# Graph attention layer with residual and layer norm, fp32: products of W and `a` spread over 14 steps, and blocks of rows that lie 32 apart

## The chip, the cores and the metric

One Trainium2 chip, one core. The time is the device time of one execution in microseconds (us), and each kernel has a median over three runs. The profile is of one further execution, with an own time and an own span (first to last instruction).

## What is computed

x is 4096 x 512, adj 4096 x 4096, W 512 x 2048 (four heads of 512), all fp32. Cut to what matters:

```python
ht = (h @ W).reshape(N, N_HEADS, N_HIDDEN).transpose(1, 0, 2)
src = jnp.einsum('hnd,hd->hn', ht, a_src)
dst = jnp.einsum('hnd,hd->hn', ht, a_dst)
e = jax.nn.leaky_relu(src[:, :, None] + dst[:, None, :], SLOPE) + adj_mat[None]
att = jax.nn.softmax(e, axis=-1)
h_prime = jnp.einsum('hij,hjd->hid', att, ht)
x = _layernorm(x + h_prime.mean(axis=0), axis=-1)
```

The entries of adj that are not zero are uniform up to 1e9, so in almost every row one entry leads the others by far more than the scores can differ. The softmax of such a row is 1 at that column, and its result is the layer norm of `x[i] + x[col(i)] @ mean over heads of W`.

## The kernel before, in words

`leading_rows` computes this short form for all rows, and a bound that proves it valid (or not) for each row. `general`, the full attention, is behind a branch on that bound; no instruction of it stands in the profiled execution.

The rows are worked on in 32 blocks of 128, one row in each of the 128 partitions; block `ib` holds rows 128*ib to 128*ib+127 (`adj_rows`, `x_rows` and `out_rows`, lines 87 to 90). A tile of adj, `adj_t`, is 128 rows of 4096 (2 MB); six buffers exist and loads run five blocks ahead (`AHEAD`). x lies in `hold`, and the result is written over it; its upper half (blocks 16 to 31) first holds W, so x groups 4 to 7 (four blocks each) can only be loaded when W has been used. A load of x takes 2 KB from each of four blocks per partition.

The loop over `t` (line 321) has one step per block. In one step:

- SP issues the load of adj for block t+5, at the steps in `x_at` a group of x before it. All loads of adj, W and x and nearly all stores stand in SP's one queue; the stores of finished groups come after the last load.
- VectorE (DVE) reduces the adj tile to 64 segment maxima in two halves (`segment_maxima`, L151). Between the halves stands `find_column` of block t-2 (it reads the gathered `lead`, and POOL then gathers the rows `y` of x), and at even t from 6 on the reciprocal of `rstd` (L213 on ScalarE, L214 and L215 on DVE) for blocks t-6 and t-5. After the second half `find_segment` finds the leading segment, and POOL gathers it (`lead`, 256 bytes a row).
- TensorE (PE) and ScalarE (ACT): `head_vector` (`vectors_at`: four at t=1 and at t=2, one at each of t=3 to 10) turns a 128 x 512 piece of W (four transposes L255), ACT copies it (`wt`, L257), and four thin products give `pv` (L259). `project` of block t-3 puts x into the accumulator `o` (L191), transposes y (L194), ACT copies (`yt`, L196), and four products with `w_sum`, the mean of the heads, add to `o` (L198). Then ACT does `finish` of two blocks (even t), `stats` of block t-4 (L208, L210) and `row_norm` (L203).

The order on every engine is the order in which the code is written (`tc.manual_schedule()`); each engine works strictly through its own list. A `rstd` on DVE at step t waits for `stats` of block t-5, which ACT did in step t-1, behind the `yt` copy of block t-4.

At t=0 PE forms `w_sum` from W (L238). After the loop stand the last columns, `test` (L296) with one product on PE, the projects of blocks 29 to 31, and the last stores.

Of the kernel before, what the change touches and what calls it, by code (L numbers as in the profile page):

```python
# [9 lines left out]
F32 = mybir.dt.float32  # L10
# [9 lines left out]
P = 128  # L20
C = 512
# [44 lines left out]
def leading_rows(ctx, tc, x, adj, W, a, out, ident, v, n_bad, any_bad):  # L66
# [3 lines left out]

    nc = tc.nc
    N, D = x.shape
    H = a.shape[0]
    KB, NB, S = D // P, N // P, N // E
    AHEAD = 5
    Q = 4
# [5 lines left out]
    rows = ctx.enter_context(tc.tile_pool(name="rows", bufs=2))  # L84
    psum = ctx.enter_context(tc.tile_pool(name="psum", bufs=4, space=bass.MemoryType.PSUM))

    adj_rows = adj.rearrange("(nb p) m -> nb p m", p=P)
    adj_segs = adj.rearrange("n (s e) -> (n s) e", e=E)
    x_rows = x.rearrange("(nb p) d -> p nb d", p=P)
    out_rows = out.rearrange("(nb p) d -> p nb d", p=P)  # L90
    w_blocks = W.rearrange("(kb p) (h d) -> p kb h d", p=P, h=H)

    hold = once.tile([P, NB, D], F32, name="hold")
# [31 lines left out]

    make_identity(nc, ident)
    first_i = once.tile([P, NB], I32, name="first_i")
    nc.gpsimd.iota(first_i, pattern=[[P * S, NB]], base=0, channel_multiplier=S)
    first = once.tile([P, NB], F32, name="first")
    nc.gpsimd.tensor_copy(first, first_i)  # L130
    ones = once.tile([P, P], F32, name="ones")
# [26 lines left out]
    def find_segment(ib):  # L158
        seg = seg_of.pop(ib)
        nc.vector.max(out=top[:, ib, :], in_=seg)  # L160
        at = small.tile([P, 8], U32, name="at")
        nc.vector.max_index(at, top[:, ib, :], seg)
        row = small.tile([P, 1], U32, name="row")
        nc.vector.tensor_tensor(row, at[:, 0:1], first[:, ib : ib + 1], op=OP.add)  # L164
        lead = small.tile([P, E], F32, name="lead")
        nc.gpsimd.indirect_dma_start(  # L166
            out=lead, out_offset=None, in_=adj_segs,
            in_offset=bass.IndirectOffsetOnAxis(ap=row[:, :1], axis=0),
        )
        at_of[ib], lead_of[ib] = at, lead  # L170
# [14 lines left out]
        )  # L185
        y_t[ib] = y

    def project(ib):
        y = y_t.pop(ib)
        o = psum.tile([P, D], F32, name="o")  # L190
        nc.tensor.matmul(o, ident, hold[:, ib, :], start=True, stop=False)  # L191
        tp = psum.tile([P, KB, P], F32, name="tp", bufs=2)
        for kb in range(KB):
            nc.tensor.transpose(tp[:, kb, :], y[:, ts(kb, P)], ident)  # L194
        yt = rows.tile([P, KB, P], F32, name="yt")
        nc.scalar.copy(yt, tp)  # L196
        for kb in range(KB):
            nc.tensor.matmul(o, yt[:, kb, :], w_sum[:, kb, :], start=False, stop=(kb == KB - 1))  # L198
        o_ps[ib] = o

    def row_norm(ib):
        sq = rows.tile([P, D], F32, name="sq")
# [9 lines left out]
    def rstd(i):  # L212
        nc.scalar.activation(sd[:, i], sd[:, i], AF.Sqrt, bias=eps, scale=1.0 / D)  # L213
        nc.vector.reciprocal(sd[:, i], sd[:, i])  # L214
        nc.vector.tensor_mul(nm[:, i], nm[:, i], sd[:, i])  # L215
# [32 lines left out]
            nc.tensor.transpose(tp[:, k, : 2 * H], a_rows[:, ts(k, P)], ident[: 2 * H, : 2 * H])  # L248
        nc.scalar.copy(at_d, tp[:, :, : 2 * H])

    def head_vector(kb, h):

        tp = psum.tile([P, KB, P], F32, name="tp", bufs=2)
        for k in range(KB):
            nc.tensor.transpose(tp[:, k, :], hold[:, w_at + kb * H + h, ts(k, P)], ident)  # L255
        wt = rows.tile([P, KB, P], F32, name="wt")
        nc.scalar.copy(wt, tp)  # L257
        for k in range(KB):
            nc.tensor.matmul(  # L259
                pv[:, kb, h : 2 * H : H], wt[:, k, :], at_d[:, k, h : 2 * H : H],  # L260
                start=(k == 0), stop=(k == KB - 1),
            )
# [47 lines left out]
        nc.vector.tensor_reduce(total, pg, axis=AX.X, op=OP.add)  # L310
        nc.vector.tensor_scalar(any_bad, total, -1.0, float(N), op0=OP.mult, op1=OP.add)

    x_at = {1: 1, 3: 2, 6: 3, 12: 4, 14: 5, 17: 6, 20: 7}
    norms_at = {t: [t - 2] for t in range(2, 18)}
    for k in range(8):
        norms_at[18 + k] = [16 + 2 * k, 17 + 2 * k]
    vectors = [(kb, h) for kb in range(KB) for h in range(H)]
    vectors_at = {1: 4, 2: 4, **{t: 1 for t in range(3, 11)}}
    COLUMN, PROJECT, STATS, FINISH = 2, 3, 4, 6

    for t in range(NB):
        if t in x_at:
            load_x(x_at[t])
        load_adj(t + AHEAD)
        segment_maxima(t, 0)
        if t >= COLUMN:
            find_column(t - COLUMN)
        if t >= FINISH and t % 2 == 0:
            rstd(slice(t - FINISH, t - FINISH + 2))
        segment_maxima(t, 1)  # L330
        find_segment(t)
        if t == 0:
            for kb in range(KB):
                mean_of_heads(kb)
            turn_a()
        for _ in range(vectors_at.get(t, 0)):
            head_vector(*vectors.pop(0))
        if t == 11:
            head_norms()
        if t >= PROJECT:  # L340
            project(t - PROJECT)
        if t >= FINISH and t % 2 == 0:
            finish(t - FINISH)
            finish(t - FINISH + 1)
        if t >= STATS:
            stats(t - STATS)
        for ib in norms_at.get(t, ()):
            row_norm(ib)
        if 27 <= t <= 29:
            bound(t - 27)  # L350

    find_column(NB - 2)
    find_column(NB - 1)
# [4 lines left out]
        store(nc.sync, g * Q, Q)  # L358
    test()
    for ib in range(NB - PROJECT, NB):  # L360
        project(ib)
        stats(ib - 1)
        rstd(slice(ib - 1, ib))
        finish(ib - 1)
        if ib == NB - 2:
            store(nc.sync, NB - Q, 2)
# [6 lines left out]
def general(ctx, tc, x, adj, W, out, ident, v, n_bad):  # L373
# [19 lines left out]
    w_blocks = W.rearrange("(kb p) m -> p kb m", p=P)  # L393

    with ExitStack() as pre:
        two = pre.enter_context(tc.tile_pool(name="two", bufs=2))
        pps = pre.enter_context(tc.tile_pool(name="pps", bufs=2, space=bass.MemoryType.PSUM))
        for g in range(NCH):
            nc.sync.dma_start(x_sb[:, ts(g, Q), :], x_blocks[:, ts(g, Q), :])
        for kb in range(KB):  # L400
            nc.sync.dma_start(w_sb[:, kb, :], w_blocks[:, kb, :])
        for g in range(NCH):
            xT = two.tile([P, KB, C], F32, name="xT")
            for q in range(Q):
                ps = pps.tile([P, KB, P], F32, name="ps_x")
                for kb in range(KB):
                    nc.tensor.transpose(ps[:, kb, :], x_sb[:, g * Q + q, ts(kb, P)], ident)
                nc.scalar.copy(xT[:, :, ts(q, P)], ps)
            ps = pps.tile([2 * H, C], F32, name="ps_sd")
            for kb in range(KB):  # L410
                nc.tensor.matmul(ps, v[:, kb, :], xT[:, kb, :], start=(kb == 0), stop=(kb == KB - 1))
            sd = two.tile([2 * H, C], F32, name="sd")
            nc.vector.tensor_copy(sd, ps)
            for h in range(H):
                pb = pps.tile([P, C], F32, name="ps_b")
                one_hot = ident[: 2 * H, H + h : H + h + 1].to_broadcast([2 * H, P])
                nc.tensor.matmul(pb, one_hot, sd, start=True, stop=True)
                nc.vector.tensor_copy(dst_b[:, h, ts(g, C)], pb)
            pt = pps.tile([P, Q, 2 * H], F32, name="ps_s")
            for q in range(Q):  # L420
                nc.tensor.transpose(pt[:, q, :], sd[:, ts(q, P)], ident[: 2 * H, : 2 * H])
            nc.vector.tensor_copy(src[:, ts(g, Q), :], pt[:, :, :H])

    adj_pool = ctx.enter_context(tc.tile_pool(name="adj_g", bufs=1))
# [7 lines left out]
    def block(ib):  # L432
        adj_t = []
        for k in range(NCH // AW):
            t = adj_pool.tile([P, AW * C], F32, name=f"adj{k}")
            nc.sync.dma_start(t, adj[ds(ib * P, P), ts(k, AW * C)])
            adj_t.append(t)
        src_i = stat.tile([P, H], F32, name="src_i", bufs=1)
        nc.vector.tensor_copy(src_i, src[:, ds(ib, 1), :].rearrange("p o h -> p (o h)"))
# [2 lines left out]
        class Unit:  # L442
# [65 lines left out]
            def project(self):  # L508
                h = self.h
                if h == 0:  # L510
                    held["o"] = psum.tile([P, D], F32, name="o_ps", bufs=1)
                for kb in range(KB):
                    nc.tensor.matmul(
                        held["o"], self.yt[:, kb, :], w_sb[:, kb, ts(h, D)],
                        start=(h == 0 and kb == 0), stop=(h == H - 1 and kb == KB - 1),
                    )

        def finish():
            r = y_pool.tile([P, D], F32, name="y_g")
            nc.vector.tensor_add(r, held["o"], x_sb[:, ds(ib, 1), :].rearrange("p o d -> p (o d)"))  # L520
            st = stat.tile([P, nc.vector.BN_STATS_DIM], F32, name="st_g")
            nc.vector.bn_stats(st, r)
            mv = stat.tile([P, nc.vector.BN_AGGR_DIM], F32, name="mv_g")
            nc.vector.bn_aggr(mv, st)
            sd = stat.tile([P, 1], F32, name="sd_g")
            nc.vector.tensor_scalar_add(sd, mv[:, 1:2], EPS)
            nc.scalar.activation(sd, sd, AF.Sqrt)
            nc.vector.reciprocal(sd, sd)
            nc.vector.tensor_scalar(r, r, mv[:, 0:1], sd, op0=OP.subtract, op1=OP.mult)
            nc.sync.dma_start(out[ds(ib * P, P), :], r)  # L530

        u = Unit(0)
        for c in range(NCH):
# [66 lines left out]
```

## Time and profile before

| | us |
|---|---|
| median of three runs (283.83, 280.98, 283.46) | 283.46 |
| the profiled execution | 282.4 |
| its span | 280.5 |
| PE busy | 220.3 |
| DVE busy | 192.1 |
| ACT busy | 120.7 |

The DMA engines moved 97.75 MB in the span, 348 GB/s on average. The mean granted clock of TensorE was 0.921 of 2.4 GHz.

How to read the rows further below: busy time alone says little, because stages have different limits. A row of the timeline gives start, duration, engine and operation, and in brackets how long the engine stood idle before it and what released it. The chain of waits follows the last instruction back to what released it, step by step; a row is start, duration and what ran. A group of instructions ends with the idle time before its members and the releaser.

### The profile page before, as it was taken

Reading aid. Unit: us, or ns where it says so; the run is one execution under the profiler, and the core shown is the slowest. Engines: PE = TensorE matmul, PEld = TensorE weight load, DVE = VectorE, ACT = ScalarE, POOL = GpSimd, SP = SyncE. Lnnn points to the kernel's source line nnn. Section 1 sums busy time; section 2 is a strip of 40 time slices with the busy share of each in tenths; the row PEclk is TensorE's granted clock in tenths of the full one; section 3 lists DMA queues with packets and bytes.
Section 4 is the critical chain, followed back from the end, with each engine's and each line's share of the span. In section 5 each row is a group of like instructions: output and inputs, shape, how many; then the busy total and the mean of one; then the engine's idle time right before and its main releaser. Section 6 shows DMA issues by size and latency. Waiting matters only on the chain.

```text
span 280.5 us, 2442 instructions
## 1 busy us (share of the span) xinstructions
PE 220.3 (79%) x683; PEld 112.6 (40%) x684; DVE 192.1 (68%) x381; ACT 120.7 (43%) x295; POOL 61.8 (22%) x75
## 2 busy tenths in 40 slices
PE   0389877778888888889987879887999789888980
PEld 0134666654444444434433333433444334343430
DVE  2524878840029695888999999599879999983011
ACT  1010211211465455365453735674566434465540
POOL 1101123310002222122332332232322322232000
PEclk9999755559999999999999997999899979999997
DMA  7999999999999979499999999999999999415121
GB/s 232 436 416 425 418 425 393 430 400 435 430 409 402 388 289 408 154 416 409 409 426 421 408 418 426 407 418 428 420 355 361 329 408 407 152 42 162 67 101 59
DMA packets 18147, 97.75 MB, mean 348 GB/s; under 512 B 1992, under 2 KB 1992, under 8 KB 13776
## 3 DMA queue, kind: packets, MB, share of 16 engines
q1 hardware_dynamic: 14384, 87.82, 77.9%
q0 software_dynamic: 3584, 9.44, 9.2%
q10 hardware_dynamic: 160, 0.28, 0.3%
q8 instruction: 7, 0.11, 0.2%
q14 instruction: 12, 0.10, 0.1%
HBM read 89.15 MB, written 8.39 MB: 348 GB/s over the span
## 4 chain that ended last, share of the span: by engine, by line
PE 43%; DMA 19%; DVE 18%; ACT 12%; issue 5%; ACTq 0%; POOLq 0%
PE o L198 19%; DVE seg L151 13%; DMA y<-in_x_dram,col 11%; PE pv L259 8%; DMA hold<-in_L_gnn_W_dram 6%; PE o L191 5%; ACT yt L196 4%; PE tp L255 4%; PE tp L194 3%; ACT wt L257 3%; PE o L238 3%; ACT sq L210 2%; DMA adj_t<-in_adj_dram 2%; ACT sq L203 2%; ACT sq L208 1%
## 5 line engine op out<-in xcount | busy, mean ns | idle before, releaser
L151 DVE TENSOR_REDUCE seg<-adj_t 128x32 f32<-128x2048 f32 (+1 forms) x68 | 146.2, 2153 | 22.9 <-DMA adj_t<-in_adj_dram 22.8
L198 PE MATMUL o<-w_sum,yt 128*128 128x512 f32 x256 | 123.4, 627 | 21.6 <-ACT yt L196 21.6
L198 PEld LDWEIGHTS o<-w_sum,yt 128*128 128x128 f32 x256 | 47.8, 197 | 78.5 <-issue 49.1
L196 ACT COPY yt<-tp 128x512 f32<-128x512 f32 x32 | 18.7, 585 | 86.0 <-PE tp L194 86.0
L166 POOL DMA_INDIRECT lead<-in_adj_dram,row x32 | 30.3, 948 | 107.8 <-DVE row L164 99.7
L182 POOL DMA_INDIRECT y<-in_x_dram,col x32 | 30.2, 944 | 85.7 <-issue 62.7
L214 DVE RECIPROCAL sd<-sd 128x2 f32<-128x2 f32 (+1 forms) x17 | 2.8, 163 | 48.7 <-ACT sd L213 48.6
L191 PE MATMUL o<-hold,ident 128*128 128x512 f32 x64 | 34.6, 623 | 0.0
L259 PE MATMUL pv<-at_d,wt 128*128 128x2 f32 x128 | 23.4, 304 | 11.3 <-ACT wt L257 11.3
L259 PEld LDWEIGHTS pv<-at_d,wt 128*128 128x128 f32 x128 | 22.0, 259 | 16.3 <-ACT wt L257 16.3
L238 PE MATMUL o<-hold,ident 128*128 128x512 f32 x32 | 15.6, 646 | 13.1 <-DMA hold<-in_L_gnn_W_dram 13.1
L194 PEld LDWEIGHTS tp<-ident,y 128*128 128x128 f32 x128 | 15.8, 143 | 25.2 <-issue 25.0
L194 PE MATMUL tp<-ident,y 128*128 128x128 f32 x128 | 19.9, 279 | 5.9 <-DMA y<-in_x_dram,col 5.9
L257 ACT COPY wt<-tp 128x512 f32<-128x512 f32 x16 | 9.4, 586 | 34.6 <-PE tp L255 34.6
L219 ACT ACTIVATE hold<-o,nm,sd 128x512 f32<-128x512 f32 x31 | 22.7, 780 | 3.0 <-DVE nm L215 3.0
L210 ACT ACTIVATE sq<-o,nm 128x512 f32<-128x512 f32 x31 | 21.3, 687 | 1.0
L203 ACT ACTIVATE sq<-hold 128x512 f32<-128x512 f32 x32 | 19.7, 619 | 0.0
L208 ACT ACTIVATE sq<-o 128x512 f32<-128x512 f32 x31 | 18.7, 603 | 0.0
L191 PEld LDWEIGHTS o<-hold,ident 128*128 128x128 f32 x64 | 11.5, 195 | 10.0 <-issue 9.9
L238 PEld LDWEIGHTS o<-hold,ident 128*128 128x128 f32 x32 | 6.5, 209 | 21.1 <-issue 18.9
L255 PE MATMUL tp<-ident,hold 128*128 128x128 f32 x64 | 13.3, 346 | 0.0
L239 ACT ACTIVATE w_sum<-o 128x512 f32<-128x512 f32 x4 | 2.4, 597 | 24.1 <-PE o L238 24.1
(66 smaller groups left out, 94.3 us busy)
## 6 DMA issues: line engine op xcount, KB each, us to landing
adj_t<-in_adj_dram SPq DMA_DIRECT2D x30, 2048.0 KB, 12.0
hold<-in_x_dram SPq DMA_DIRECT2D x8, 1024.0 KB, 15.8
out_dram<-hold SPq DMA_DIRECT2D x7, 1024.0 KB, 14.3
adj_t<-in_adj_dram SPq DMA_DIRECT2D x8, 512.0 KB, 6.5
hold<-in_L_gnn_W_dram SPq DMA_DIRECT2D x4, 1024.0 KB, 10.6
lead<-in_adj_dram,row POOLq DMA_INDIRECT x32, 6.4
y<-in_x_dram,col POOLq DMA_INDIRECT x32, 7.2
out_dram<-hold SPq DMA_DIRECT2D x1, 512.0 KB, 2.8
```

Source lines behind the costliest of these rows:

```text
L151: nc.vector.tensor_reduce(seg_of[ib][:, ts(k, S // n)], adj_t[ib][:, ts(k, N // n)].rearrange("p (s e) -> p s e", e=E), axis=AX.X, op=OP.max,)
L166: nc.gpsimd.indirect_dma_start(out=lead, out_offset=None, in_=adj_segs, in_offset=bass.IndirectOffsetOnAxis(ap=row[:, :1], axis=0),)
L182: nc.gpsimd.indirect_dma_start(out=y, out_offset=None, in_=x, in_offset=bass.IndirectOffsetOnAxis(ap=col[:, :1], axis=0),)
L191: nc.tensor.matmul(o, ident, hold[:, ib, :], start=True, stop=False)
L194: nc.tensor.transpose(tp[:, kb, :], y[:, ts(kb, P)], ident)
L196: nc.scalar.copy(yt, tp)
L198: nc.tensor.matmul(o, yt[:, kb, :], w_sum[:, kb, :], start=False, stop=(kb == KB - 1))
L203: nc.scalar.activation(sq, hold[:, ib, :], AF.Square, accum_out=xx[:, ib : ib + 1])
L210: nc.scalar.activation(sq, o, AF.Square, bias=nm[:, i], accum_out=sd[:, i])
L238: nc.tensor.matmul(o, ident, hold[:, w_at + kb * H + h, :], start=(h == 0), stop=(h == H - 1))
L255: nc.tensor.transpose(tp[:, k, :], hold[:, w_at + kb * H + h, ts(k, P)], ident)
L259: nc.tensor.matmul(pv[:, kb, h : 2 * H : H], wt[:, k, :], at_d[:, k, h : 2 * H : H], start=(k == 0), stop=(k == KB - 1),)
```

## The change

Four things change in `leading_rows`:

1. Layout: block `ib` holds rows ib, ib+32, ib+64 and so on; partition p holds rows 32p to 32p+31. A load of an adj tile takes 128 rows of 16 KB that lie 512 KB apart; before, they were one run of 2 MB. A load of a group of x and a store of a group take one run of 8 KB per partition, not four of 2 KB.
2. `head_vector` is split: `turn_w` (transposes and copy) stands at the start of PE's part of a step, the thin products stand inside `project`. There are two at t=1 and 2, and one at each of t=3 to 14. The steps of x loads (`x_at`), of `head_norms` (11 to 16), of `row_norm` in pairs (18 to 20) and of `bound` (27 to 28) move too.
3. `project` transposes y first, and the product that puts x into `o` stands behind the copy of `yt`; for the last block alone it stays first.
4. `rstd` stands after both halves of the segment maxima and `find_segment`.

```diff
-    adj_rows = adj.rearrange("(nb p) m -> nb p m", p=P)
+    adj_rows = adj.rearrange("(p nb) m -> nb p m", nb=NB)
...
-    x_rows = x.rearrange("(nb p) d -> p nb d", p=P)
-    out_rows = out.rearrange("(nb p) d -> p nb d", p=P)
+    x_rows = x.rearrange("(p nb) d -> p nb d", nb=NB)
+    out_rows = out.rearrange("(p nb) d -> p nb d", nb=NB)
...
-    nc.gpsimd.iota(first_i, pattern=[[P * S, NB]], base=0, channel_multiplier=S)
+    nc.gpsimd.iota(first_i, pattern=[[S, NB]], base=0, channel_multiplier=NB * S)
...
-    def project(ib):
+    def project(ib, between=(), wait=False):
+
+        o = o_ps[ib] = psum.tile([P, D], F32, name="o")
+
+        def residual():
+            nc.tensor.matmul(o, ident, hold[:, ib, :], start=True, stop=False)
+
+        if wait:
+            residual()
         y = y_t.pop(ib)
-        o = psum.tile([P, D], F32, name="o")
-        nc.tensor.matmul(o, ident, hold[:, ib, :], start=True, stop=False)
         tp = psum.tile([P, KB, P], F32, name="tp", bufs=2)
...
         nc.scalar.copy(yt, tp)
+        if not wait:
+            residual()
+        for some in between:
+            head_vector(*some)
         for kb in range(KB):
             nc.tensor.matmul(o, yt[:, kb, :], w_sum[:, kb, :], start=False, stop=(kb == KB - 1))
...
-    def head_vector(kb, h):
-
+    def turn_w(kb, h):
...
+        return wt
+
+    def head_vector(kb, h, wt):
+
...
-    x_at = {1: 1, 3: 2, 6: 3, 12: 4, 14: 5, 17: 6, 20: 7}
+    x_at = {1: 1, 4: 2, 8: 3, 11: 4, 14: 5, 18: 6, 21: 7}
...
-    vectors_at = {1: 4, 2: 4, **{t: 1 for t in range(3, 11)}}
+    vectors_at = {t: 2 if t < 3 else 1 for t in range(1, 15)}
...
-        if t >= FINISH and t % 2 == 0:
-            rstd(slice(t - FINISH, t - FINISH + 2))
         segment_maxima(t, 1)
         find_segment(t)
+        pair = t >= FINISH and t % 2 == 0
+        if pair:
+            rstd(slice(t - FINISH, t - FINISH + 2))
...
-        for _ in range(vectors_at.get(t, 0)):
-            head_vector(*vectors.pop(0))
-        if t == 11:
+        turned = [(*vectors[0], turn_w(*vectors.pop(0))) for _ in range(vectors_at.get(t, 0))]
+        if t == 16:
             head_norms()
...
         if t >= PROJECT:
-            project(t - PROJECT)
+            project(t - PROJECT, turned)
+        else:
+            for some in turned:
+                head_vector(*some)
...
-        project(ib)
+        project(ib, wait=(ib == NB - 1))
```

`general` follows the new layout (its parts of the diff are left out here).

PE's list from the eighth vector on, before (L255 and L259 are a vector, L191, L194 and L198 a project):

```order
L255 MATMUL tp<-ident,hold 128x128 x4
L259 MATMUL pv<-at_d,wt 128x2 x4
L191 MATMUL o<-hold,ident 128x512
L194 MATMUL tp<-ident,y 128x128 x4
L198 MATMUL o<-w_sum,yt 128x512 x4
L255 MATMUL tp<-ident,hold 128x128 x4
L259 MATMUL pv<-at_d,wt 128x2 x4
L191 MATMUL o<-hold,ident 128x512
L194 MATMUL tp<-ident,y 128x128 x4
L198 MATMUL o<-w_sum,yt 128x512 x4
```

The same list after, from the first vectors on (L264 and L272 are a vector, L201, L194 and L209 a project):

```order
L264 MATMUL tp<-ident,hold 128x128 x8
L272 MATMUL pv<-at_d,wt 128x2 x8
L264 MATMUL tp<-ident,hold 128x128 x8
L272 MATMUL pv<-at_d,wt 128x2 x8
L264 MATMUL tp<-ident,hold 128x128 x4
L201 MATMUL tp<-ident,y 128x128 x4
L194 MATMUL o<-hold,ident 128x512
L272 MATMUL pv<-at_d,wt 128x2 x4
L209 MATMUL o<-w_sum,yt 128x512 x4
L264 MATMUL tp<-ident,hold 128x128 x4
L201 MATMUL tp<-ident,y 128x128 x4
```

Before the first project there now stand four vectors and the transposes of a fifth, where nine stood; between a transpose and the product that needs its copy there now stands other work.

DVE's list in step 6, before, from the first half of the tile to the second:

```order
L151 TENSOR_REDUCE seg<-adj_t 128x32
L174 MAX inner<-lead 128x8
L176 MAX_INDEX within<-inner,lead 128x8
L178 SCALAR_TENSOR_TENSOR col<-at,within 128x1
L214 RECIPROCAL sd<-sd 128x2
L215 TENSOR_TENSOR nm<-nm,sd 128x2
L151 TENSOR_REDUCE seg<-adj_t 128x32
```

The same step after, from the column to the first half of the next tile:

```order
L179 SCALAR_TENSOR_TENSOR col<-at,within 128x1
L152 TENSOR_REDUCE seg<-adj_t 128x32
L161 MAX top<-seg 128x8
L163 MAX_INDEX at<-top,seg 128x8
L165 TENSOR_TENSOR row<-at,first 128x1
L224 RECIPROCAL sd<-sd 128x2
L225 TENSOR_TENSOR nm<-nm,sd 128x2
L152 TENSOR_REDUCE seg<-adj_t 128x32
```

The reciprocal that waits for ACT moved behind one half of the tile and the search for its segment.

## Rows read from the trace of the kernel before

**Rows 1.** The page, the span in 40 slices of 7.01 us.

```profile
PEclk9999755559999999999999997999899979999997
DMA  7999999999999979499999999999999999415121
GB/s 232 436 416 425 418 425 393 430 400 435 430 409 402 388 289 408 154 416 409 409 426 421 408 418 426 407 418 428 420 355 361 329 408 407 152 42 162 67 101 59
```

**Rows 2.** Groups by form: busy us, mean ns | idle us before them, releaser.

```profile
L198 PE MATMUL o<-w_sum,yt 128*128 128x512 f32 x256 | 123.4, 627 | 21.6 <-ACT yt L196 21.6
...
L259 PE MATMUL pv<-at_d,wt 128*128 128x2 f32 x128 | 23.4, 304 | 11.3 <-ACT wt L257 11.3
...
L214 DVE RECIPROCAL sd<-sd 128x2 f32<-128x2 f32 x14 | 2.3, 163 | 34.7 <-ACT sd L213 34.6
```

**Rows 3.** Timeline of DVE around its longest wait: start us, us, operation.

```profile
60.39 0.16 DVE L178 SCALAR_TENSOR_TENSOR col<-at,within 128x1 uint32<-128x1 uint32 x1
82.51 0.17 DVE L214 RECIPROCAL sd<-sd 128x2 f32<-128x2 f32 x1 [21.96 <-ACT sd L213]
...
82.79 2.28 DVE L151 TENSOR_REDUCE seg<-adj_t 128x32 f32<-128x2048 f32 x1
...
85.77 2.28 DVE L151 TENSOR_REDUCE seg<-adj_t 128x32 f32<-128x2048 f32 x1
...
91.61 2.28 DVE L151 TENSOR_REDUCE seg<-adj_t 128x32 f32<-128x2048 f32 x1
```

**Rows 4.** Chain of waits, 36 to 75 us: start us, us, what.

```profile
36.34 1.87 PE pv L259 x8
...
66.67 0.45 PE tp L255 x4
...
67.84 1.05 PE pv L259 x8
68.89 0.97 PE o L191 x2
...
70.33 0.59 ACT yt L196
70.97 3.70 PE o L198 x8
74.67 0.45 PE tp L255 x4
```

**Rows 5.** Chain of waits, 139 to 152 us: from a gather of y to DVE.

```profile
139.92 7.61 DMA y<-in_x_dram,col
147.66 0.64 PE tp L194 x4
...
151.50 2.21 DVE seg L151
```

**Rows 6.** Chain of waits, from 250 us to the end.

```profile
250.36 0.31 DVE at L162 x2
251.12 2.37 DMA lead<-in_adj_dram,row
...
255.78 1.05 PE o L191 x2
...
269.29 3.71 PE o L198 x8
273.03 0.71 DVE st L224
```

**Rows 7.** The page, DMA queues: packets, MB, share of 16 engines.

```profile
q1 hardware_dynamic: 14384, 87.82, 77.9%
q0 software_dynamic: 3584, 9.44, 9.2%
```

**Rows 8.** The page, DMA issues: us from issue to landing (median).

```profile
lead<-in_adj_dram,row POOLq DMA_INDIRECT x32, 6.4
y<-in_x_dram,col POOLq DMA_INDIRECT x32, 7.2
```

More of the change, by code (lines that the diff above doesn't have):

```diff
@@ L196, in project @@
         nc.scalar.copy(yt, tp)
+        if not wait:
+            residual()
+        for some in between:
+            head_vector(*some)
         for kb in range(KB):
             nc.tensor.matmul(o, yt[:, kb, :], w_sum[:, kb, :], start=False, stop=(kb == KB - 1))
-        o_ps[ib] = o
     def row_norm(ib):
@@ L311, in test @@
         nc.vector.tensor_scalar(any_bad, total, -1.0, float(N), op0=OP.mult, op1=OP.add)
-    x_at = {1: 1, 3: 2, 6: 3, 12: 4, 14: 5, 17: 6, 20: 7}
+    x_at = {1: 1, 4: 2, 8: 3, 11: 4, 14: 5, 18: 6, 21: 7}
     norms_at = {t: [t - 2] for t in range(2, 18)}
     for k in range(8):
-        norms_at[18 + k] = [16 + 2 * k, 17 + 2 * k]
+        norms_at[20 + k] = [16 + 2 * k, 17 + 2 * k]
     vectors = [(kb, h) for kb in range(KB) for h in range(H)]
-    vectors_at = {1: 4, 2: 4, **{t: 1 for t in range(3, 11)}}
+    vectors_at = {t: 2 if t < 3 else 1 for t in range(1, 15)}
     COLUMN, PROJECT, STATS, FINISH = 2, 3, 4, 6
@@ L335, in leading_rows @@
             turn_a()
-        for _ in range(vectors_at.get(t, 0)):
-            head_vector(*vectors.pop(0))
-        if t == 11:
+        turned = [(*vectors[0], turn_w(*vectors.pop(0))) for _ in range(vectors_at.get(t, 0))]
+        if t == 16:
             head_norms()
+        if 28 <= t <= 30:
+            bound(t - 28)
         if t >= PROJECT:
-            project(t - PROJECT)
-        if t >= FINISH and t % 2 == 0:
+            project(t - PROJECT, turned)
+        else:
+            for some in turned:
+                head_vector(*some)
+        if pair:
             finish(t - FINISH)
@@ L348, in leading_rows @@
             row_norm(ib)
-        if 27 <= t <= 29:
-            bound(t - 27)
     find_column(NB - 2)
@@ L395, in general @@
     with ExitStack() as pre:
+        sd_all = pre.enter_context(tc.tile_pool(name="all", bufs=1)).tile([2 * H, N], F32, name="sd_all")
         two = pre.enter_context(tc.tile_pool(name="two", bufs=2))
@@ L411, in general @@
                 nc.tensor.matmul(ps, v[:, kb, :], xT[:, kb, :], start=(kb == 0), stop=(kb == KB - 1))
-            sd = two.tile([2 * H, C], F32, name="sd")
+            sd = sd_all[:, ts(g, C)]
             nc.vector.tensor_copy(sd, ps)
@@ L418, in general @@
                 nc.vector.tensor_copy(dst_b[:, h, ts(g, C)], pb)
+        for g in range(NCH):
             pt = pps.tile([P, Q, 2 * H], F32, name="ps_s")
             for q in range(Q):
-                nc.tensor.transpose(pt[:, q, :], sd[:, ts(q, P)], ident[: 2 * H, : 2 * H])
+                rows_of = sd_all[:, ds(g * Q + q, P, NB)]
+                nc.tensor.transpose(pt[:, q, :], rows_of, ident[: 2 * H, : 2 * H])
             nc.vector.tensor_copy(src[:, ts(g, Q), :], pt[:, :, :H])
@@ L435, in block @@
             t = adj_pool.tile([P, AW * C], F32, name=f"adj{k}")
-            nc.sync.dma_start(t, adj[ds(ib * P, P), ts(k, AW * C)])
+            nc.sync.dma_start(t, adj[ds(ib, P, NB), ts(k, AW * C)])
             adj_t.append(t)
@@ L519, in finish @@
             r = y_pool.tile([P, D], F32, name="y_g")
-            nc.vector.tensor_add(r, held["o"], x_sb[:, ds(ib, 1), :].rearrange("p o d -> p (o d)"))
+            nc.sync.dma_start(r, x[ds(ib, P, NB), :])
+            nc.vector.tensor_add(r, r, held["o"])
             st = stat.tile([P, nc.vector.BN_STATS_DIM], F32, name="st_g")
@@ L529, in finish @@
             nc.vector.tensor_scalar(r, r, mv[:, 0:1], sd, op0=OP.subtract, op1=OP.mult)
-            nc.sync.dma_start(out[ds(ib * P, P), :], r)
+            nc.sync.dma_start(out[ds(ib, P, NB), :], r)
         u = Unit(0)
```

## The prediction, made before the changed kernel was run

> **What bounds the kernel now.** I read the slices of the page first, then the groups with their idle times, the timeline of VectorE (DVE) around its longest wait, and the chain of waits. In the slices [rows 1] the reader is to see a DMA stream that is full from the second slice on, but for a dip to 289 and one to 154 GB/s (slices 15 and 17, some 98 to 119 us), and that ends about 240 us; 40 us of tail follow with little traffic. So two things cost time beyond the stream: the dips, and the tail.
>
> The dips start on DVE. At 60.55 us it has the column of tile 4 and comes to the reciprocal of the first `rstd`, where it stands idle for 21.96 us until ACT delivers [rows 3]. Loads of adj wait for DVE to free a buffer, so the stream runs dry some 40 us later, when five tiles of lead are used up. ACT is late because TensorE (PE) is late: nine vectors stand ahead of its first project, each with two waits for a copy by ACT, and the clock in slices 6 to 9 of the PEclk row is at half, 1.2 of 2.4 GHz [rows 1]; the products of one vector take 1.87 us there, against 1.05 us later [rows 4]. The 14 pair-wise reciprocals of the loop wait 34.6 us for ACT in all [rows 2]; less the first, 12.6 us are spread over the others.
>
> From 82.5 us on DVE is the pace: a step without `rstd` is 5.84 us (85.77 to 91.61), one with it 0.28 us more (82.51 to 82.79) [rows 3], and DVE reads its last segment at 250.36 + 0.31 = 250.67 us [rows 6].
>
> **The first rstd (parts 2 to 4 of the change).** After W's mean, PE now has four vectors before the first project, not eight and one more. At the slow clock a vector is about 0.97 + 0.6 + 1.87 = 3.5 us (its products from [rows 4], its transposes at twice the 0.45 us there), so four end about 29 + 14 = 43 us, about when the first y lands; the first project comes at 43 us, not 59. A round of one vector and one project was 8.00 us (66.67 to 74.67 [rows 4]). Now both copies by ACT are covered: the `wt` copy by the transposes of y, the `yt` copy by the product of x (0.97 us) and the vector's products. Left are 0.45 (transposes of W) + 0.47 (of y) + 0.97 + 1.05 + 3.70 = 6.64 us. Project 1 ends near 43 + 1.5 (clock still low) + 2 x 6.64 = 58 us, and ACT's stats of it, behind the next `yt` copy, near 62 us. DVE reaches its `rstd` at 60.55 + 2.28 + 0.75 (half a tile, the search) = 63.6 us. So the 21.96 us go.
>
> Twelve such rounds at 6.64 us against DVE's 5.84 + 0.14 = 5.98 us let PE fall behind by up to 12 x 0.66 = 8 us; the slack above and the DMA's own pace (below) take most of it, and I count a remainder of up to 3 us. From step 15 on a project is 5.12 us of PE, and it catches up. `head_norms` at step 16 comes after the last vector and adds nothing to before.
>
> **The later rstds (part 4).** From the issue of a gather of y to the next reduction behind the `rstd` it holds up are 151.50 - 139.92 = 11.6 us [rows 5], plus 0.8 us from DVE's column to the issue. Before, DVE had two steps for that, 11.7 to 12.0 us; a gather a little slow stalled it. Now `rstd` comes 2.28 + 0.75 = 3.0 us later in the step, and the 12.6 us go too. What queues behind it: ACT's `finish` of the pair comes 3 us later, behind it `stats`, `row_norm` and the next square root, some 3 us before DVE asks for it; the four accumulators are free in time. PE now waits for y ahead of x's product and the vector's products; a late y delays these too, 2.0 us a round, inside the slack of a step once the vectors are done.
>
> So DVE alone could read its last segment at 250.67 - 21.96 - 12.6 = 216.1 us, or 219 with PE's 3 us.
>
> **What is late next: the stream.** By 56.1 us the first eight slices have moved 3175 x 7.01 = 22.3 MB [rows 1]. Until the last adj tile lands, 67.1 (adj) + 8.4 (x) + 4.2 (W) + 8.9 (gathers, 15/16 of q0's 9.44 [rows 7]) = 88.6 MB must have gone. The mean of slices 2 to 14 is 416 GB/s, so the last tile lands at 56.1 + 66.3/0.416 = 215.5 us; a quarter tile and the search take DVE 1.9 us more: 217.4. Two limits so near each other cost something jointly; I take 219 us. The moved loads of x keep their number and the queue; adj tiles 8 to 10 come a little earlier for it, x is needed later than it lands.
>
> **The new layout (part 1).** No row shows adj rows 512 KB apart, so bounds: nothing, as the loads of x before already take 2 KB pieces from four places 256 KB apart and their slices stay near 416 GB/s; at the other end the rate of the gathers, the most scattered traffic there is. q1 moves 87.82 MB in 77.9% of 16 x 280.5 us, 25.1 GB/s per engine, q0 22.9 [rows 7], a ratio of 0.91: adj's 161 us at 416 GB/s would become 177, +16 us. I take +3 us, near the x loads, which are of the same queue and kind. Longer runs of x and of the result could gain: slices 30 to 32, with stores, move a mean of 348 GB/s [rows 1]; at 416 the result's 8.4 MB take 20 us, not 24. But the stores stand behind the last load and end before the tail does, so the 4 us are cover, not path; for x I allow up to 2 us of gain in the lower bound.
>
> The Trainium skill has a rule against this part. DMA: Bandwidth & Descriptors, section "Latency and other measured facts", reports copies of tiles of 128 rows of 16 KiB between HBM tensors: 207 GB/s each way at a row pitch of 512 KiB, 214 at a pitch that is no large power of two, and less at pitches of 2 MiB and more. As an estimate by that page, adj would lose 3.4%, 5.5 us where I take 3. Whether a stream of loads alone at 416 GB/s suffers as little the page does not say, and no run here shows it yet.
>
> **The tail.** From DVE's last segment (250.67) to the end of the span are 29.8 us: gather of the lead (2.37 us [rows 6]), column, test, three projects from 255.78 to 273.0 [rows 6], last norm and store. Before, the queues were empty there. Now the loads end at 216 us and most of 7 MB of stores still stand behind them, so the lead takes its loaded 6.4 us [rows 8]: +4.0. Two of the three projects hide the `yt` copy, 0.64 us each (269.29 to 273.0 is the products alone; before them 0.6 of waiting): -1.3; the last keeps the old order.
>
> **Sum.** 219 + 3 = 222 us for the last segment; 222 + 29.8 + 4.0 - 1.3 = 254.5 us of span; the profiled execution lasted 282.4 for a span of 280.5, so 256.4 us, against its own 282.4. That execution is 1.1 us under the median of the three runs, within their spread of 2.9 us. I say 256.
>
> **The rivals.**
>
> *Gathers come too late (264 to 277 us).* From a search to the use of its lead DVE leaves one step and half a tile, 5.98 + 2.28 = 8.3 us; 0.3 us go before the issue, and the landing takes 6.4 us at the median [rows 8]. Now 128 segments lie 512 KB apart with nearly equal offsets, and the stream never pauses. If a landing takes 8.8 us, DVE's step grows by 0.8 us, some 20 us over 25 steps: 276; half of that 266. For: 1.6 us of room is little. Against: before, DVE waited for a lead once in the loop's whole length, at its end. A half clock on PE at the y waits would cost about as much.
>
> *Slower: adj rows 512 KB apart cost bandwidth (296 us).* The place is the one DMA queue from the first tile to the last. Were adj to run at the worst full slice, 329 GB/s [rows 1], 67.1 MB take 204 us instead of 161, +43 where I counted 3: 296. It decides from about 345 GB/s down, where adj takes 194 us and what the rest gains is used up. For: sixteen engines then work at addresses that differ by multiples of a power of two, all through. Against: the strided x loads show no such loss. Beside it, the Trainium skill (DMA: Bandwidth & Descriptors, "Latency and other measured facts"): its 207 GB/s, read as a cap on loads too, would give as an estimate 324 us for adj alone; that page's copies at a harmless pitch go no faster than 214, which speaks against that reading.
>
> *Nothing moves (282 us).* PE stays late for `rstd` and DVE waits elsewhere. For: PE is the busiest engine. Against: the sum of 6.64 us and the earlier start, both from rows.
>
> **How the numbers follow.** Forecast (247 to 264) 0.69; gathers late 0.17; nothing moves 0.05; slower 0.09. Low end: DVE's 216.1 + 29.8 - 1.3 + 1.9 = 246.5, no price for layout or loaded lead. High end: +16 instead of +3 gives 269, and a part of the late gathers reaches 273. Faster by over 1% is the first two, 0.86; a difference of 1% (2.8 us) is about what these runs can tell. Within 1%: 0.05. Slower: 0.09.
>
> **What would show it.** Right: DVE's wait before the first reciprocal under 2 us and the pair-wise ones under 5 us in all; the slices near 416 GB/s without a dip to 215 to 220 us; DVE idle now for adj tiles; PE's waits for `yt` and `wt` nearly gone; a vector round of about 6.6 us; the last search near 222 us. Wrong: adj slices under 400 GB/s with DVE waiting for adj (layout), DVE waiting for lead (gathers), or PE's clock at half beyond 62 us.

## The result and the profile after

| | before | after |
|---|---|---|
| median us of four executions (lowest to highest) | 283.39 (280.98 to 283.83) | 257.4 (255.93 to 257.6) |
| the profiled execution | 282.4 | 257.6 |
| its span | 280.5 | 255.8 |

The ratio is 0.9088, with an interval of 0.9026 to 0.9149; 256 us was forecast, in a range of 247 to 264. Each kernel below is given as a ratio to the kernel before, run beside it on its own chip.

The page after, in 40 slices of 6.4 us (to be read against [rows 1]):

```profile
PEclk9999975799999999999959999999979999995997
DMA  6999999999999999999999999999999999975021
GB/s 247 439 411 433 423 421 434 412 423 427 419 416 425 425 416 431 418 417 421 427 420 423 423 423 414 425 428 418 419 428 416 418 402 427 423 311 206 15 108 53
```

There is no dip any more: every slice from the second to the 35th moves over 400 GB/s. The mean of slices 2 to 14 is 424 GB/s, where it was 416.

Groups by form, idle time before them behind the bar (against [rows 2]):

```profile
L209 PE MATMUL o<-w_sum,yt 128*128 128x512 f32 x256 | 123.3, 626 | 0.7 <-ACT yt L203 0.7
...
L272 PE MATMUL pv<-at_d,wt 128*128 128x2 f32 x128 | 16.4, 252 | 0.5 <-ACT wt L266 0.5
...
L224 DVE RECIPROCAL sd<-sd 128x2 f32<-128x2 f32 x14 | 2.2, 158 | 0.0
```

The 14 pair-wise reciprocals, which waited 34.6 us, wait for nothing; PE's waits for the two copies fell from 21.6 and 11.3 us to 0.7 and 0.5.

PE's timeline over a round of a vector and a project, to the start of the next (against [rows 4]), and DVE's at the first `rstd` (against [rows 3]):

```profile
49.96 0.60 PE L264 MATMUL tp<-ident,hold 128*128 128x128 f32 x4
50.39 0.60 PE L201 MATMUL tp<-ident,y 128*128 128x128 f32 x4
50.83 1.02 PE L194 MATMUL o<-hold,ident 128*128 128x512 f32 x2
51.69 0.95 PE L272 MATMUL pv<-at_d,wt 128*128 128x2 f32 x8
52.50 3.68 PE L209 MATMUL o<-w_sum,yt 128*128 128x512 f32 x8
56.02 0.60 PE L264 MATMUL tp<-ident,hold 128*128 128x128 f32 x4
```

```profile
59.41 0.16 DVE L179 SCALAR_TENSOR_TENSOR col<-at,within 128x1 uint32<-128x1 uint32 x1
...
62.47 0.16 DVE L224 RECIPROCAL sd<-sd 128x2 f32<-128x2 f32 x1
```

A round is 56.02 - 49.96 = 6.06 us, not 8.00. The reciprocal has no idle time in brackets: the 21.96 us are gone. What DVE waits for from 60 us to the last search, from the waits of that stretch (us in total, times, longest):

```profile
DVE seg L152 <- DMA adj_t<-in_adj_dram: 6.8, 5, 1.6
DVE n L284 <- PE px L282: 0.8, 1, 0.8
```

It now waits for adj tiles, five times, the last time at 185 us. Before the change it waited for none behind 60 us.

The chain of waits from the last search to the end (against [rows 6]):

```profile
221.42 0.31 DVE at L163 x2
...
222.18 5.70 DMA lead<-in_adj_dram,row
...
229.94 0.27 PE px L320 x2
230.21 1.05 PE tp L201 x4
231.25 1.71 PE o L194 x2
232.96 5.03 PE o L209 x8
237.99 0.44 PE tp L201 x4
238.43 0.86 PE o L194 x2
239.29 3.52 PE o L209 x8
...
248.51 0.71 DVE st L234
```

The last search ends at 221.73 us; 222 was forecast. The tail is 34.1 us, against 29.8 before. The lead takes 5.70 us behind the stores. The first project after the test takes 7.8 us (230.21 to 237.99) and the next one 4.8: PE had stood idle 4.6 us for the test's product, and the granted clock falls to half in the slice of 230 us. Before, PE stood idle only 0.68 us there, and a project of the tail took 5.67 us. The test's product after the change, and before:

```profile
229.94 0.27 PE L320 MATMUL px<-gap,ones 128*1 128x32 f32 x2 [4.64 <-DVE gap L318]
```

```profile
255.56 0.22 PE L307 MATMUL px<-gap,ones 128*1 128x32 f32 x2 [0.68 <-DVE gap L305]
```

Two starts of projects in the chain before, 5.67 us apart:

```profile
261.65 0.86 PE o L191 x2
...
267.32 0.86 PE o L191 x2
```

### The profile page after: what moved, and what is told of

The parts are those of the page before. It is cut to its first block, busy times and chain, and to the rows that moved or that the text cites. A ratio compares the mean times of both kernels' runs of the same rounds, so it can differ in the third digit from the quotient of the medians.

```text
span 255.8 us, 2438 instructions
## 1 busy us (share of the span) xinstructions
PE 209.2 (82%) x683; PEld 106.1 (41%) x684; DVE 191.7 (75%) x381; ACT 120.0 (47%) x295; POOL 61.8 (24%) x75
## 4 chain that ended last, share of the span: by engine, by line
DMA 55%; DVE 33%; PE 7%; issue 1%; SPq 1%; ACT 0%
DMA adj_t<-in_adj_dram 53%; DVE seg L152 24%; PE o L209 5%; DMA lead<-in_adj_dram,row 2%; DVE within L177 2%; PE o L194 1%; DVE at L163 1%; DVE top L161 1%; DVE inner L175 1%; DVE col L179 1%; PE tp L201 1%; DVE row L165 1%; SPq L106 1%; DVE nm L225 0%; DVE hold L240 0%
## 5 line engine op out<-in xcount | busy, mean ns | idle before, releaser
L209 PE MATMUL o<-w_sum,yt 128*128 128x512 f32 x256 | 123.3, 626 | 0.7 <-ACT yt L203 0.7
L209 PEld LDWEIGHTS o<-w_sum,yt 128*128 128x128 f32 x256 | 48.9, 200 | 63.9 <-issue 51.1
L194 PE MATMUL o<-hold,ident 128*128 128x512 f32 x64 | 36.3, 652 | 0.0
L201 PE MATMUL tp<-ident,y 128*128 128x128 f32 x128 | 21.3, 292 | 16.8 <-DMA y<-in_x_dram,col 16.7
L201 PEld LDWEIGHTS tp<-ident,y 128*128 128x128 f32 x128 | 15.2, 149 | 29.5 <-issue 26.8
L248 PE MATMUL o<-hold,ident 128*128 128x512 f32 x32 | 17.1, 702 | 11.4 <-DMA hold<-in_L_gnn_W_dram 11.4
L272 PEld LDWEIGHTS pv<-at_d,wt 128*128 128x128 f32 x128 | 17.6, 204 | 7.3 <-issue 3.6
L272 PE MATMUL pv<-at_d,wt 128*128 128x2 f32 x128 | 16.4, 252 | 0.5 <-ACT wt L266 0.5
L175 DVE MAX8 inner<-lead 128x8 f32<-128x64 f32 x32 | 6.9, 217 | 5.3 <-DMA lead<-in_adj_dram,row 5.3
L194 PEld LDWEIGHTS o<-hold,ident 128*128 128x128 f32 x64 | 10.7, 208 | 0.5 <-issue 0.5
```

Source lines behind the costliest of these rows:

```text
L248: nc.tensor.matmul(o, ident, hold[:, w_at + kb * H + h, :], start=(h == 0), stop=(h == H - 1))
L272: nc.tensor.matmul(pv[:, kb, h : 2 * H : H], wt[:, k, :], at_d[:, k, h : 2 * H : H], start=(k == 0), stop=(k == KB - 1),)
```

## Experiments

**Order of work alone, layout alone.** The changed kernel with the four lines of the old layout, and the old kernel with those of the new one:

```diff
-    adj_rows = adj.rearrange("(p nb) m -> nb p m", nb=NB)
+    adj_rows = adj.rearrange("(nb p) m -> nb p m", p=P)
...
```

> The changed order of work with the old layout of rows. Theory: nearly all of the 26 us come from the order, and the layout costs nothing, since the stream moved a mean of 423 GB/s in slices 2 to 14 after the change against 416 before. The loads of x go back to 2 KB pieces, so the stream should lose a little: 258 to 261 us. Rival 1 (the prediction's term: rows 512 KB apart cost 3 us): 254 to 255 us. Rival 2 (the layout brings a good part of the gain): over 265 us.

> The old order of work with the new layout of rows. Theory: before, VectorE's waits for the first normalisation and not the stream set the pace, so a stream that is a little better or worse changes nothing: 281 to 285 us, with the wait of some 22 us before the first reciprocal still there. Rival 1 (the wide pitch costs): 286 us or more. Rival 2 (the layout brings a good part of the gain): under 275 us.

Order alone: 260.1 us (259.33 to 260.78), ratio 0.9198 (0.9138 to 0.9258). Layout alone: 282.7 us, ratio 0.9968 (0.9914 to 1.0022), no difference that can be measured, and its first reciprocal waits 23.5 us:

```profile
83.53 0.17 DVE L214 RECIPROCAL sd<-sd 128x2 f32<-128x2 f32 x1 [23.48 <-ACT sd L213]
```

So the order brings 8 of the 9%. With the new order the layout helps by about 1%: from 60 to 180 us the stream moves 422 GB/s with it and 417 without, and the last search ends at 221.7 and 224.8 us. That 1% is near the limit of what the runs can tell, since the intervals of the two ratios still touch.

**Loads alone.** All but the loads, a read of one column of each tile and the stores is taken out, in each layout.

> Only the loads of adj, W and x in the new layout, with VectorE reading one column of each tile, and stores of what lies in the buffer; all the rest is left out. Theory: adj rows 512 KB apart stream as fast as contiguous tiles, 415 to 430 GB/s: 80 MB in some 190 us, then 20 us of stores: 208 to 218 us. Rival (the pitch is hidden in the whole kernel but costs by itself): 225 us or more.

> The kernel of loads alone with the old layout of rows; the rest is left out as in its twin, which took 215.1 us and moved 426 GB/s from 10 to 190 us. Theory (the pitch costs nothing and the 2 KB pieces of x a little): 216 to 220 us and 418 to 425 GB/s. Rival (the wide pitch costs 1% or more): under 213 us.

215.1 us new and 218.3 us old, one execution each. From 10 to 190 us, the last column of the windows, first the new layout, then the old:

```profile
10.00:190.00 180.00, 0.00 (x0) 4.92 (x32) 0.00 (x0) 0.00 (x0) 1.00 1.01 426
```

```profile
10.00:190.00 180.00, 0.00 (x0) 4.76 (x31) 0.00 (x0) 0.00 (x0) 1.00 1.01 422
```

Rows of 16 KB that lie 512 KB apart cost nothing here. The two differ by the pitch of adj and by the pieces of x and of the result (8 or 2 KB) together; that the longer pieces bring the 3 us is argued from this, not isolated.

**rstd back between the halves.**

```diff
-        segment_maxima(t, 1)
-        find_segment(t)
         pair = t >= FINISH and t % 2 == 0
         if pair:
             rstd(slice(t - FINISH, t - FINISH + 2))
+        segment_maxima(t, 1)
+        find_segment(t)
```

> The changed kernel with the reciprocal of rstd back between the two halves of a tile. Theory: from a column to the reciprocal that its y holds up there are some 12 to 13 us (0.8 to the issue, 8.3 landing, 3 to 4 on TensorE and ScalarE) against two steps of 12.0 us; each of 13 pairs stalls VectorE by about 1 us, of which its 7 us of waits for adj after 60 us hide a part: 262 to 268 us, with 10 to 20 us of waits of the pair-wise reciprocals. Rival (the stalls came from TensorE's backlog alone, and the place of rstd does not matter): 257 to 258.5 us.

259.5 us (259.12 to 260.51), ratio 0.9181 (0.9119 to 0.9243): a smaller loss than expected, and its interval still touches that of the changed kernel. The row by form:

```profile
L224 DVE RECIPROCAL sd<-sd 128x2 f32<-128x2 f32 x14 | 2.3, 164 | 7.5 <-ACT sd L223 7.4
```

The waits are there, 7.4 us, but in exchange DVE waits less for adj. From 60 to 225 us:

```profile
DVE sd L224 <- ACT sd L223: 7.4, 9, 1.4
DVE seg L152 <- DMA adj_t<-in_adj_dram: 1.2, 2, 0.8
```

6.8 us of waits for adj became 1.2, so 7.4 + 1.2 - 6.8 = 1.8 us of it count, about the difference of the medians, 2.1 us.

**rstd late in the kernel before**, the same move in the other direction and nothing else:

> The kernel before with rstd behind both halves and the search, nothing else changed. Theory: the later stalls (12.6 us) go and the first becomes 3 us shorter: 266 to 273 us, with a first wait of about 19 us. Rival (TensorE's backlog and not the place sets those stalls): 278 to 284 us.

277.1 us, ratio 0.9805 (0.9749 to 0.9862), between what was expected and the rival. DVE's timeline, the first four reciprocals:

```profile
84.43 0.17 DVE L214 RECIPROCAL sd<-sd 128x2 f32<-128x2 f32 x1 [20.82 <-ACT sd L213]
...
98.90 0.17 DVE L214 RECIPROCAL sd<-sd 128x2 f32<-128x2 f32 x1 [2.42 <-ACT sd L213]
...
114.78 0.17 DVE L214 RECIPROCAL sd<-sd 128x2 f32<-128x2 f32 x1 [3.85 <-ACT sd L213]
...
131.00 0.16 DVE L214 RECIPROCAL sd<-sd 128x2 f32<-128x2 f32 x1
```

The waits while vectors still run (20.82 + 2.42 + 3.85 = 27.1 us) stay; those behind them are gone. Of the 34.6 us of [rows 2] the place of `rstd` is worth 34.6 - 27.1 = 7.5 us, the same size as the 7.4 us above; the medians differ by 5.3 us.

**Vectors early, in the new order inside a round.** Four at steps 1 and 2, in pairs, and one at steps 3 to 10:

```diff
-    vectors_at = {t: 2 if t < 3 else 1 for t in range(1, 15)}
+    vectors_at = {1: 4, 2: 4, **{t: 1 for t in range(3, 11)}}
...
```

> The changed kernel with four vectors at steps 1 and 2 and one at steps 3 to 10, as before the change. Theory: four vectors more at the slow clock ahead of the first project, 2 x 3.6 us each pair as the trace after shows them, delay it by some 7 us, and VectorE waits 5 to 12 us for the first rstd; later rounds and the five tiles of lead give most of that back: 257 to 262 us. Rival (the early vectors alone made the 22 us of before): the wait is back at about 20 us and the time at 265 us or more.

257.1 us (256.52 to 257.42), ratio 0.9113 (0.9064 to 0.9162): the same as the changed kernel. From 60 us to the last search, of the reciprocals only the first waits:

```profile
DVE sd L224 <- ACT sd L223: 6.1, 1, 6.1
```

In exchange the 6.8 us of waits for adj are gone, and the last search ends at 222.6 us, not 221.7. Within the new round the spread over 14 steps brings nothing more.

**Old order inside a round, with the spread.** x's product first, a vector's products right behind its copy:

```diff
-        if wait:
-            residual()
+        residual()
...
-        if not wait:
-            residual()
-        for some in between:
-            head_vector(*some)
...
```

> The changed kernel with the old order inside a project and a vector: x's product first, nothing between a transpose and the product that needs its copy. The spread over 14 steps stays. Theory: a round of vector and project takes 8.0 us, not 6.1, against VectorE's 6.0, so TensorE falls some 20 us behind in twelve rounds and the reciprocals wait for it: 266 to 276 us. Rival (the earlier first project and the later rstd are what counts): 257 to 260 us.

269.0 us (268.26 to 270.46), ratio 0.9541 (0.9479 to 0.9603). PE's timeline of one round:

```profile
60.21 0.60 PE L259 MATMUL tp<-ident,hold 128*128 128x128 f32 x4
61.48 1.05 PE L267 MATMUL pv<-at_d,wt 128*128 128x2 f32 x8 [0.68 <-ACT wt L261]
62.40 1.10 PE L194 MATMUL o<-hold,ident 128*128 128x512 f32 x2
63.34 0.60 PE L200 MATMUL tp<-ident,y 128*128 128x128 f32 x4
64.61 3.70 PE L204 MATMUL o<-w_sum,yt 128*128 128x512 f32 x8 [0.68 <-ACT yt L202]
68.15 0.60 PE L259 MATMUL tp<-ident,hold 128*128 128x128 f32 x4
```

Both waits for a copy are back, the round is 68.15 - 60.21 = 7.94 us, and the reciprocals wait 5.6, 2.4 and four times 1.6 to 3.9 us:

```profile
L219 DVE RECIPROCAL sd<-sd 128x2 f32<-128x2 f32 x14 | 2.3, 162 | 21.1 <-ACT sd L218 21.1
```

Taken back by itself, the order inside a round is the largest part, 11.6 us. The runs also make a ladder: `rstd` late brings the kernel before from 282.4 to 277.1 us; the spread, with the new layout and the moved steps, to 269.0; the order inside a round to 257.4. In the old round the first wait falls from 20.8 to 5.6 us with the second of these steps, and layout alone had moved nothing, so most of its 8.1 us are likely the spread; no run has the spread alone there. What the spread is worth thus hangs on the round: up to 8 us in the old one, nothing in the new.

**The tail: the test's product later.** The product stands behind the project of block 30:

```diff
...
-    test()
+    gap = test()
     for ib in range(NB - PROJECT, NB):
+        if ib == NB - 1:
+            count(gap)
```

> The changed kernel with the product of the test moved on TensorE behind the project of block 30. Theory: TensorE stood 4.6 us at that product while y of block 29 had landed at about 226.6 us, and then ran at half the clock for 8 us; the project of block 29 starts 3.5 us earlier and without the slow stretch (about 3 us): 250.5 to 253 us. Rival (y of block 31, which lands near 236 us, or the stores set the end): 256 to 257.5 us.

256.8 us (255.37 to 257.31), ratio 0.9079 (0.9019 to 0.9138): a miss. The timeline shows a new wait in the old one's place:

```profile
227.87 0.63 PE L201 MATMUL tp<-ident,y 128*128 128x128 f32 x4 [1.69 <-DMA y<-in_x_dram,col]
...
228.75 0.23 DVE L175 MAX8 inner<-lead 128x8 f32<-128x64 f32 x1 [5.25 <-DMA lead<-in_adj_dram,row]
...
229.81 1.45 ACT L229 ACTIVATE hold<-o,nm,sd 128x512 f32<-128x512 f32 x2 [5.65 <-DVE nm L225]
...
231.14 0.58 ACT L203 COPY yt<-tp 128x512 f32<-128x512 f32 x1
```

PE has transposed y by 228.5 us, but ACT copies it at 231.14: `finish` of blocks 26 and 27 stands ahead, whose scale DVE computes only behind its 5.25 us of waiting for the last lead.

**That wait removed too.** The last pair-wise `rstd` and its `finish` go ahead of the last column:

```diff
     find_column(NB - 2)
-    find_column(NB - 1)
     rstd(slice(NB - FINISH, NB - FINISH + 2))
     finish(NB - FINISH)
     finish(NB - FINISH + 1)
+    find_column(NB - 1)
```

> The changed kernel with the product of the test behind the project of block 30, and the last pair-wise rstd and its finish ahead of the last column. Theory: moving the test alone gained little because ScalarE's copy of y of block 29 then stood behind the finish of blocks 26 and 27, whose scale VectorE computed only after it had waited 5.3 us for the last lead; with both moved that copy runs at 228.5 us, not 231.1, and the products 2.4 us earlier: 253.5 to 255.5 us. Rival (something else late, as y of block 30 or 31): 256 to 257.5 us.

252.1 us (251.95 to 252.42), ratio 0.8946 (0.8877 to 0.9015), below the expected range and better than both kernels. Its timeline:

```profile
223.80 1.45 ACT L229 ACTIVATE hold<-o,nm,sd 128x512 f32<-128x512 f32 x2 [0.43 <-DVE nm L225]
...
226.89 0.63 PE L201 MATMUL tp<-ident,y 128*128 128x128 f32 x4 [1.50 <-DMA y<-in_x_dram,col]
...
227.56 0.59 ACT L203 COPY yt<-tp 128x512 f32<-128x512 f32 x1 [2.31 <-PE tp L201]
```

`finish` runs at 223.80, the copy at 227.56, and PE goes from project to project: with an idle stretch of 1.50 us ahead, not 4.6, the first runs at full speed.

**Stores held back**, alone and with the edit above; the store of group 6, which waits for blocks 26 and 27, stands first:

```diff
-    for g in range(NB // Q - 1):
+    for g in (6, 0, 1, 2, 3, 4, 5):
```

> The changed kernel with the store of group 6, which waits for the last pair, ahead of the stores of groups 0 to 5, so that no store is on the way while the last lead and the last y are gathered. Theory (the tail's term: the lead takes 6 us behind stores, 2.4 without): the last lead lands 3 us earlier, and so do the test and the last projects; the 7 MB of stores take 18 us and end before the last one: 253 to 255.5 us. Rival (held stores end later than the tail and cost as much): 257 to 262 us.

> Both edits of the tail together. Theory: the two gains overlap in part, since both shorten the way from the last segment to the project of block 29: 251.5 to 254.5 us. Rival: no better than the better one of the two.

255.8 us (ratio 0.9073, 0.9004 to 0.9143), short of what was expected, and 253.8 us (0.9001, 0.893 to 0.9073), in the expected range but worse than the 252.1 us without the held stores: the rival was right there. The chain of the first:

```profile
222.32 2.42 DMA lead<-in_adj_dram,row
...
226.82 0.22 PE px L320 x2
...
242.52 0.71 DVE st L234
```

```profile
DMA  7999999999999999999999999999999995139993
```

The lead lands in 2.42 us, and the last norm starts at 242.52 us, 6.0 us earlier than in the changed kernel (248.51). But the stores now fill the DMA engines to the end, and the last store stands among them: from the end of the last norm to the end of the span 8.6 us pass, not 5. So 6.0 us won on the chain become 2.4 us of span (255.8 to 253.4), and 1.6 us in the medians. With both edits it is the same: the last norm starts at 241.1 us, 1.6 us earlier than with the tail's order alone, and 8.5 us follow its end, not 5.

## Why the prediction was right, point by point

- **The first rstd.** Right: 21.96 us became nothing, and DVE came to it at 62.5 us (63.6 forecast). On PE the four vectors took 6.7 us, not 14: done in pairs they waited for a copy only 0.18 and 0.30 us, and the granted clock was 0.98 from 28 to 35 us, where the sum took half. The first project then waited 3.93 us for its y, to 40.45 us (43 forecast). Two remedies stand in this part and either is nearly enough: with the old round and the spread the wait is 5.6 us, with the new round and no spread 6.1 us. The working uses both and gives neither a price of its own; once the copies are covered the spread is worth nothing, and with the spread in place covering them is still worth 11.6 us.
- **The round.** 6.64 us was forecast, 6.06 us measured. The step that was off is the sum of durations: 1.05 and 3.70 us are of groups that began after a wait, and without the wait each group starts 0.14 to 0.17 us before the former has ended (transposes 0.43, x's product 0.86, thin products 0.81, products 3.52 us from start to start). With 6.06 us PE fell behind DVE hardly at all, and the 3 us counted for it were not needed.
- **The later rstds.** The 12.6 us went, but the step that gave them all to the place of `rstd` was off by half: with the place alone 2.42 + 3.85 = 6.3 us of them stayed, and belong to the long rounds. On the changed kernel the place is worth only 2 us of time, because DVE would else wait for adj.
- **What is late next.** Right: DVE waits for adj, the stream is even, and the last search came at 221.73 us for 222. The joint price of two limits so near each other was sized too low, though: about 2 us were taken, and DVE lost 6.8 us to adj after 60 us that it never got back, since from 185 us on it was the slower one itself. That made up for the 3 us of PE and the 3 us of layout, which were not needed; that 222 was met to 0.3 us is in part luck.
- **The layout.** Here the term had the wrong sign: +3 us was taken, and with the new order the layout is worth about 2.7 us (260.1 to 257.4). The strided loads of x had been the right neighbour, and the gathers the wrong end. One row was misread: slices 30 to 32 before the change are not slow for their stores alone, since the first store is issued at 215.0 us, in slice 31; slice 30, at 355 GB/s, holds none. And the upper bound of 16 us leads to 269 us, beyond the 264 at which the forecast ends. For copies at a row pitch of 512 KiB the Trainium skill (DMA: Bandwidth & Descriptors, "Latency and other measured facts") has 207 GB/s each way against 214. This loss of 3.4% does not carry over to loads alone: 426 GB/s at that pitch, 422 without it. Neither does the reading of 207 GB/s as a cap.
- **The tail.** The loaded lead was forecast at +4.0 and measured +3.3 us. The hidden copies gave 5.67 to 4.81 us for a project (0.64 forecast, 0.86 measured), but PE's idle 4.6 us at the test's product cost the first project 3.0 us at the lower clock, which the sum did not have; the tail is 34.1 us for 32.5 forecast.
- **The rivals.** Gathers did not come too late: a lead landed in 6.7 us at the median and 8.1 at most, and DVE waited for one only once, the last. PE waited 16.7 us for y in all (5.9 before), but no pair-wise reciprocal waited for that.

The kernel is now held by stream and DVE at once until 222 us, and then by a chain of single waits; the best version here takes 5 us from that chain.

## What to carry to other kernels

Where a matrix product needs a copy of a transpose, put another product between them on the engine: covering 0.68 us twice in each of twelve rounds was worth 11.6 us. Two remedies for one wait don't add up: spreading the work was worth up to 8 us while the copies were uncovered and nothing afterwards, so take each back by itself before you credit it. An engine that works strictly in order hands one late wait on to everybody behind it, so of each wait that is moved ask what stands next in every list; one of the two tail edits alone gained almost nothing, both gained 5 us. A layout that only helps the stream can show its worth only when the stream is the limit: here nothing before the other edits, about 1% behind them.

## What the runs showed of the hardware that was not expected

Loads of 16 KB rows 512 KB apart ran at 426 GB/s over 180 us, no slower than contiguous tiles (422 GB/s). After PE had stood idle 4.6 us at full clock, its next project took 7.8 us, not 4.8; after 1.5 us idle it took 4.84 us (226.89 to 231.73, in the run with the tail's order). The changed kernel has two more such stretches: after 3.11 us idle a project took 7.6 us (127.86 to 135.48), after 2.26 us idle 6.5 us (184.45 to 190.91). Nor does a busy PE always hold its clock: with the vectors early it was busy throughout from 33 to 47 us, on transposes and products of two columns alone, and the granted clock was 0.50.
